# Where an expert's second bias is added: a row matmul on TensorE, or an add on VectorE

## The chip, the cores and the metric

The kernel runs on one core of a Trainium2 chip, in one launch. The metric is the device time in microseconds of an execution; the time shown is the median of three. Besides, one execution was taken by the hardware profiler. Engines are named as in the profile: PE is TensorE's matmuls and PEld its weight loads, DVE is VectorE, ACT is ScalarE, POOL is GpSimd, SP is SyncE. A float32 matmul shows as two rows in the profile.

## The reference

One layer of a graph network over 6250 nodes of 256 features with 206250 edges. The sum of an edge attention (8 heads, softmax over a node's incoming edges) and a linear attention is added to the input; the result is normalised, and a mixture of 8 experts with top-1 routing and a capacity is added. Cut to the part that matters here:

```python
xn = _layernorm(x)
x  = x + gnn(xn, edges) + mix(xn)
h  = _layernorm(x)
probs = softmax(h @ gate_w + gate_b); idx = argmax(probs); prb = probs[idx]
# each token goes to its expert's buffer while there is room (C places)
hmid = relu(einsum('ecd,edf->ecf', buf, w1) + b1[:, None, :])      # 256 -> 1024
ybuf = einsum('ecf,efd->ecd', hmid, w2) + b2[:, None, :]           # 1024 -> 256
x  = x + nan_to_num(ybuf[idx, pos] * (prb * kept))
```

`b2` is the second bias: one row of 256 numbers for each expert, added to every token's result before it is scaled by the token's gate.

## The kernel before

Nodes are sorted by degree and lie in 49 blocks of 128, in three groups of 21, 17 and 11 blocks (`GROUPS`). A key-value table is written first. Then comes the main loop, over the blocks of all groups: each block is cut into units of at most about 20 edge slots, each unit into chunks of 4 or 5 slots. For a chunk, GpSimd gathers 4 or 5 rows of the table for each node (line 662, tile `kvg`, a ring of 10 buffers). VectorE multiplies the keys by the query (line 1620) and reduces to scores (line 1621). When a unit's scores are complete ScalarE takes the exponentials (line 1652, tile `pr`), and while the next unit's chunks are scored, VectorE weights the values of this one (`weigh`, line 1549) and TensorE sums them with an identity matrix into `pa` (line 1553). At a block's end the sum is divided (line 1586) and goes through the output projection, a normalisation and the gate (`out_step`, lines 897 to 952).

All other work is made of Python generators. `background(n)` in the main loop is called twice per chunk with a credit of slots, and takes steps from the first job in `jobs` until the credit is used. Each step says by its `yield` how much it cost. So the engines' queues are written out by hand: where a generator yields is where the attention's instructions come in between, on every engine. A block's own output steps are taken from `outs`.

When all blocks of a group are through, `behind(g)` routes its tokens (`routing`, `to_tiles`) into tiles of one expert each, and `experts(g)` computes them while the next group's attention runs. In the first two groups a tile has 256 rows, two halves of 128 (`SUB` = 2), with 18 and 16 tiles: 34 tiles, 68 halves. In the last group a tile has 128 rows, and there is no attention beside it. Tiles are worked in phases; a phase (0, t) turns the rows and computes `hidden` (line 1369, then the Relu with the first bias on ScalarE at line 1375), a phase (1, t) computes `final`: for each half k, eight matmuls (line 1386) add up in one bank of PSUM, `py`, written out in two parts of four with a yield between. Both parts are followed by `step()`, which takes one step of every open `close`.

`close(t, k, ...)` ends a half: it makes the result tile `res` (pool `d2`, two buffers), scales it by the gate on ScalarE (line 1403, which also leaves a sum for the check on finite numbers), waits some steps, adds the residual rows `xt` on VectorE (line 1406), and one step later stores it, in the first two groups on SyncE to `rbuf` (line 1410). As `final` appends a new `close` to `closing` right ahead of `step()`, its first piece is written out directly after the half's last matmul. The weights `w2_t` (tile `wt`, pool `d3`, three buffers) carry behind them the expert's bias, repeated in all 128 partitions.

The bias comes in one of two ways. In the first two groups a ninth matmul (line 1392) multiplies a row of ones by one row of the bias and adds it to `py`. In the last group, where `last` holds, VectorE adds it (line 1400) before ScalarE scales, and a yield stands between the two.

Of the kernel before, what the change touches and what calls it, by code (L numbers as in the profile page):

```python
# [18 lines left out]
P = 128  # L19
# [51 lines left out]
def gps_layer(  # L71
# [36 lines left out]
    nc = tc.nc  # L108
    N, D = x.shape
# [13 lines left out]
    FC = F // P  # L123
# [33 lines left out]
    with tc.manual_schedule():  # L157
# [12 lines left out]
        ones = keep.tile([P, 8 * max(GROUPS)], F32, name="ones")  # L170
# [52 lines left out]
        def bank(shape):  # L223

            t = bps.tile([P, 512], F32, name="bank")
            n = math.prod(shape)
            v = t[:, :n]
            if len(shape) == 2:
                v = v.rearrange("p (a b) -> p a b", a=shape[0])
            if len(shape) == 3:  # L230
                v = v.rearrange("p (a b c) -> p a b c", a=shape[0], b=shape[1])
            return v
# [616 lines left out]
        def spaced_scatter(key, **kw):  # L849

            s = nc.gpsimd.indirect_dma_start(**kw)
            for other in sent.setdefault(key, []):
                tc.declare_no_dep(s.ins, other.ins, reason="each token has a row of its own")
            sent[key].append(s)
            gap = keep.tile([P, 1], F32, name="gap")
            nc.gpsimd.memset(gap, 0.0)
# [425 lines left out]
        def experts(gi):  # L1282
# [5 lines left out]
            last = gi == NG - 1  # L1288
# [3 lines left out]
            V2 = FC * D  # L1292
# [86 lines left out]
            def final(t, k, part):  # L1379
                w2_t = T[t][1]  # L1380
                w = w2_t[:, :V2].rearrange("p (f d) -> p f d", f=FC)
                if part == 0:
                    T[t]["py"] = bank((D,))
                py = T[t]["py"]
                for f in range(part * FC // 2, (part + 1) * FC // 2):
                    nc.tensor.matmul(  # L1386
                        py, T[t]["hT"][:, f, k * P : (k + 1) * P], w[:, f, :], start=(f == 0),
                        stop=(last and f == FC - 1),
                    )
                if part == 1:  # L1390
                    if not last:
                        nc.tensor.matmul(py, ones[:1, :P], w2_t[:1, V2 : V2 + D], start=False, stop=True)  # L1392
                    closing.append(close(t, k, py, T[t]["xt"][k], w2_t[:, V2 : V2 + D]))

            def close(t, k, py, xt, b2_t):

                f = sum(NSUB[:gi]) + t * SUB + k
                res = d2.tile([P, D], F32, name="res")
                if last:
                    nc.vector.tensor_add(res, py, b2_t)  # L1400
                    py = res
                    yield
                nc.scalar.activation(res, py, AF.Copy, scale=xt[:, D : D + 1], accum_out=finite[:, f : f + 1])  # L1403
                for _ in range(1 if last else 3):
                    yield
                nc.vector.tensor_add(res, res, xt[:, :D])  # L1406
                yield
                if not last:
                    r0 = (t * SUB + k) * P
                    nc.sync.dma_start(rbufs[gi][r0 : r0 + P, :], res)  # L1410
                    return
                spaced_scatter(
                    "out", out=out[:, :],
                    out_offset=bass.IndirectOffsetOnAxis(ap=xt[:, D + 1 :].bitcast(I32), axis=0),
                    in_=res, in_offset=None, bounds_check=N - 1, oob_is_err=False,
                )
# [8 lines left out]
            f = 1.0  # L1425

            def run():
# [19 lines left out]
                for i, (which, t) in enumerate(phases):  # L1447
                    load_w(i + AHEAD)
                    if which == 0:
                        if t > n_begin:  # L1450
                            load(t - 1, "xt", slice(D, XW))
                        for fa in range(0, FC, 2):
                            hidden(t, fa)
                            step()
                            yield 0.9 * SUB * f
                        T[t].pop("xT")
                        turn(t + 1)
                        load_x(t + 2)
                        yield 0.4 * SUB * f
                    else:  # L1460
                        if t == n_end - 1:
                            load(t, "xt", slice(D, XW))
                        for k in range(SUB):
                            for part in range(2):
                                final(t, k, part)
                                step()
                                yield 2.0 * f
                        T[t].clear()
# [755 lines left out]
```

## Time and profile before

| what | value |
|---|---|
| time, median of 3 | 3196.92 us (3190.28 to 3212.74) |
| profiled execution, its own time | 3236.41 us |
| its span | 3234.6 us |
| mean granted TensorE clock | 0.834 |
| busy, PE / DVE / ACT / POOL | 70 / 68 / 24 / 58% of the span |
| L1392, the row matmul | 136 rows of 432 ns (median), two for each of 68 |
| L1403, the scaling, read from PSUM | 68 of 474 ns (median) |
| L1400, the bias add of the last group | 11 of 425 ns (median) |
| L1406, the residual add | 79 of 419 ns (median) |

The times of the table's last four lines are those of the views of these lines. The profile's views read as follows. A group's line gives line, engine, operation, result and operands, then busy time, the mean of one, and the idle time of the engine ahead of it with what ended it. A view of a line gives the least, median and largest duration, who it waited for and who waited for it. A view of stretches gives for each its length, the busy time of each engine with the number of its instructions, and at the end the granted TensorE clock, the DMA engines' share and GB/s. The timeline gives start, length, and in brackets the engine's idle time before. Consecutive rows of one kind are merged there, and rows of different engines overlap.

### The profile page before, as it was taken

To read this page: it belongs to the slowest core of one execution; us is meant where nothing else is said; L and a number is where in the kernel's file an instruction comes from. 1 tells how busy PE (TensorE), PEld (TensorE's weight loads), DVE (VectorE), ACT (ScalarE), POOL (GpSimd) and SP (SyncE) were. 2 spreads that over 40 slices of the span, in tenths; PEclk is the share of its full clock that TensorE was granted. 3 is DMA by queue.
4 is the path that set the end of the run, shared out by engine and by line. 5 is a ranking of instruction groups with operands and counts; after the bars stand their busy time and mean duration, and the time that the engine had idled before them with its cause. 6 is when DMAs were issued, how large, how long until landed. Compare 5 with 4: busy or idle time off the path is not lost. (4 is left out here: it accounts for less than half of the span.)

```text
span 3234.6 us, 29841 instructions
## 1 busy us (share of the span) xinstructions
PE 2256.7 (70%) x8968; PEld 1725.6 (53%) x8968; DVE 2185.8 (68%) x3637; ACT 767.9 (24%) x2022; POOL 1870.4 (58%) x2026
## 2 busy tenths in 40 slices
PE   7635577767777566674468888878745479998847
PEld 3324344545544454553357777666634357776637
DVE  4758788878788577786557667666767546766631
ACT  4200233333333122220012222222210112222213
POOL 4356666666666655655656666656665655665411
PEclk9857788888888788886679998988976689998969
DMA  6556677777776666665767877777664778887475
GB/s 229 183 164 182 210 224 226 226 220 225 222 214 191 190 191 200 205 180 149 256 212 258 262 251 262 245 237 238 209 184 157 249 233 270 288 272 253 155 257 214
DMA packets 257274, 710.88 MB, mean 220 GB/s; under 512 B 42183, under 2 KB 92113, under 8 KB 245580
## 3 DMA queue, kind: packets, MB, share of 16 engines
q0 software_dynamic: 148880, 477.59, 48.6%
q1 hardware_dynamic: 108220, 231.24, 20.2%
q8 instruction: 76, 1.25, 0.2%
q14 instruction: 98, 0.80, 0.1%
HBM read 626.63 MB, written 82.06 MB: 219 GB/s over the span
## 5 line engine op out<-in xcount | busy, mean ns | idle before, releaser
L662 POOL DMA_INDIRECT kvg<-kv_tab,idx x1714 | 1628.6, 950 | 1080.2 <-issue 470.8
L1553 PE MATMUL pa<-kvg,ident 128*128 128x256 f32 x3428 | 1012.1, 451 | 577.0 <-DVE kvg L1549 367.8
L1553 PEld LDWEIGHTS pa<-kvg,ident 128*128 128x128 f32 x3428 | 755.7, 227 | 794.4 <-DVE kvg L1549 407.3
L1620 DVE TENSOR_TENSOR kvg<-kvg,qc 128x1024 f32<-128x1024 f32 (+1 forms) x381 | 514.0, 1349 | 116.0 <-issue 69.2
L1621 DVE TENSOR_REDUCE sim<-kvg 128x32 f32<-128x1024 f32 (+1 forms) x381 | 515.4, 1353 | 18.2 <-remote 4.1
L1549 DVE TENSOR_TENSOR kvg<-kvg,pr 128x1024 f32<-128x1024 f32 (+1 forms) x381 | 510.4, 1343 | 0.0
L1369 PE MATMUL bank<-xTe,wt 128*128 128x256 f32 x1088 | 265.4, 391 | 29.2 <-ACT xTe L1359 15.7
L1386 PE MATMUL bank<-wt,hTe 128*128 128x256 f32 x1088 | 274.8, 399 | 14.9 <-issue 14.7
L1386 PEld LDWEIGHTS bank<-wt,hTe 128*128 128x128 f32 x1088 | 216.8, 202 | 52.1 <-issue 21.2
L1369 PEld LDWEIGHTS bank<-xTe,wt 128*128 128x128 f32 x1088 | 210.7, 197 | 61.8 <-issue 16.9
L1375 ACT ACTIVATE hTe<-bank,wt 128x256 f32<-128x256 f32 x272 | 113.2, 473 | 372.8 <-PE bank L1369 137.1
L756 PE MATMUL bank<-wm,xTm 128*128 128x512 f32 x392 | 185.8, 617 | 3.4 <-issue 3.3
L1560 DVE TENSOR_REDUCE s<-pr 128x8 f32<-128x120 f32 (+8 forms) x108 | 30.5, 282 | 156.6 <-ACT pr L1652 103.3
L756 PEld LDWEIGHTS bank<-wm,xTm 128*128 128x128 f32 x392 | 75.3, 203 | 79.5 <-issue 79.2
L1403 ACT ACTIVATE res<-bank,xt 128x256 f32<-128x256 f32 x68 | 32.2, 474 | 349.0 <-PE bank L1392 183.4
L1578 DVE TENSOR_TENSOR acc<-acc,pa 128x256 f32<-128x256 f32 x59 | 24.9, 421 | 124.7 <-remote 94.2
L548 PE MATMUL pkv<-wn,xT 128*128 128x512 f32 x196 | 95.0, 637 | 16.8 <-DVE kv L562 12.2
L765 ACT ACTIVATE sq<-bank 128x512 f32<-128x512 f32 x98 | 55.5, 594 | 186.1 <-remote 87.9
L785 ACT ACTIVATE ck<-bank,rk 128x64 f32<-128x64 f32 x392 | 86.6, 350 | 30.5 <-issue 15.6
L896 PE MATMUL bank<-ident,qs 128*128 128x128 f32 x56 | 15.0, 358 | 102.3 <-DVE qs L1586 57.6
L773 DVE TENSOR_REDUCE rv<-sq 128x16 f32<-128x1024 f32 x49 | 59.4, 1213 | 38.9 <-ACT sq L765 36.7
L1406 DVE TENSOR_TENSOR res<-res,xt 128x256 f32<-128x256 f32 x79 | 33.3, 421 | 70.2 <-ACT res L1403 41.1
(312 smaller groups left out, 2471.3 us busy)
## 6 DMA issues: line engine op xcount, KB each, us to landing
wt<-in_w_rows_dram SPq DMA_DIRECT2D x34, 1152.0 KB
wt<-in_w_rows_dram SPq DMA_DIRECT2D x34, 1028.0 KB
kvg<-kv_tab,idx POOLq DMA_INDIRECT x1714
xbuf<-zero SPq DMA_DIRECT2D x43, 514.0 KB
kvg<-in_w_rows_dram SPq DMA_DIRECT2D x11, 1152.0 KB
kv_tab<-kv SPq DMA_DIRECT2D x49, 256.0 KB
hx_tab<-hx SPq DMA_DIRECT2D x49, 256.0 KB
kvg<-in_w_rows_dram SPq DMA_DIRECT2D x11, 1028.0 KB
```

Source lines behind the costliest of these rows:

```text
L548: nc.tensor.matmul(done[b], xTs[b // GX][:, b % GX, c, :], wn[:, c, :], start=(c == 0), stop=(c == DC - 1))
L662: nc.gpsimd.indirect_dma_start(out=kv[:, j - j0, :], out_offset=None, in_=kv_tab[:, :], in_offset=bass.IndirectOffsetOnAxis(ap=idx_of[b][: ...
L756: nc.tensor.matmul(pm, xT_of[b][:, c, :], wmf[:, c, s * MI : (s + 1) * MI], start=(c == 0), stop=(c == DC - 1),)
L773: nc.vector.tensor_reduce(rv, sqs[b], AX.X, ALU.add)
L785: nc.scalar.activation(cks[b][:, h, :], pms[b][0][:, h * MD : (h + 1) * MD], AF.Copy, scale=rk[:, h : h + 1])
L1369: nc.tensor.matmul(ph[:, k, :], w[:, c, f * P : (f + 1) * P], T[t]["xT"][:, c, :size], start=(k == 0 and c == 0), stop=(k == 1 and c == DC ...
L1375: nc.scalar.activation(T[t]["hT"][:, f, :size], ph[:, k, :], AF.Relu, bias=w1_t[:, V1 + f : V1 + f + 1])
L1386: nc.tensor.matmul(py, T[t]["hT"][:, f, k * P : (k + 1) * P], w[:, f, :], start=(f == 0), stop=(last and f == FC - 1),)
L1549: nc.vector.tensor_tensor(vals, vals, v["pr"][:, j0 - s0 : j1 - s0, :, None].to_broadcast([P, m, GH, GD]), ALU.mult)
L1553: nc.tensor.matmul(v["pa"], ident, kv[:, j, D:], start=(j0 + j == s0), stop=(j0 + j == s1 - 1),)
L1620: nc.vector.tensor_tensor(keys, keys, qc[:, None, :].to_broadcast([P, j1 - j0, D]), ALU.mult)
L1621: nc.vector.tensor_reduce(sim[:, j0 - s0 : j1 - s0, :], keys.rearrange("p j (h d) -> p j h d", d=GD), AX.X, ALU.add)
```

## The change

The ninth matmul goes, and `close` adds the bias on VectorE in all groups, as the last group did already; the yield between the add and ScalarE's scaling comes with it. ScalarE then reads `res` instead of PSUM. All that follows in `close` is written out one step later. The adds of the last group stay as they were.

```diff
                 for f in range(part * FC // 2, (part + 1) * FC // 2):
                     nc.tensor.matmul(
                         py, T[t]["hT"][:, f, k * P : (k + 1) * P], w[:, f, :], start=(f == 0),
-                        stop=(last and f == FC - 1),
+                        stop=(f == FC - 1),
                     )
                 if part == 1:
-                    if not last:
-                        nc.tensor.matmul(py, ones[:1, :P], w2_t[:1, V2 : V2 + D], start=False, stop=True)
                     closing.append(close(t, k, py, T[t]["xt"][k], w2_t[:, V2 : V2 + D]))
 
             def close(t, k, py, xt, b2_t):
 
                 f = sum(NSUB[:gi]) + t * SUB + k
                 res = d2.tile([P, D], F32, name="res")
-                if last:
-                    nc.vector.tensor_add(res, py, b2_t)
-                    py = res
-                    yield
+                nc.vector.tensor_add(res, py, b2_t)
+                py = res
+                yield
                 nc.scalar.activation(res, py, AF.Copy, scale=xt[:, D : D + 1], accum_out=finite[:, f : f + 1])
                 for _ in range(1 if last else 3):
                     yield
                 nc.vector.tensor_add(res, res, xt[:, :D])
                 yield
```

## The prediction

> **What bounds the kernel now.** I read the page first, for the totals; then the busy time in the two stretches in which the first two groups' experts run (they are where the page's lines L1369 and L1386 work on `wt`); then the row matmul's own view; then the timeline around single closes, because busy shares cannot show who waits for whom. By "close" I mean the end of one 128-row result, 68 of them in the first two groups.
>
> ```profile
> span 3234.6 us, 29841 instructions
> PE 2256.7 (70%) x8968; PEld 1725.6 (53%) x8968; DVE 2185.8 (68%) x3637; ACT 767.9 (24%) x2022; POOL 1870.4 (58%) x2026
> 1690.00:2340.00 650.00, 547.12 (x2349) 446.51 (x2348) 449.11 (x649) 147.53 (x355) 404.45 (x427) 0.92 0.76 245
> 2600.00:3060.00 460.00, 412.05 (x1805) 338.81 (x1806) 291.31 (x419) 112.12 (x281) 257.01 (x272) 0.94 0.75 250
> ```
>
> The columns of the last two lines are length, PE, PEld, DVE, ACT, POOL, then the granted clock. In these 1110 us TensorE is busy 959 us and idle only 151; VectorE is busy 740 and idle 370. Over the whole span the two look alike (70% and 68%); here TensorE is the tight engine. So on shares alone this change is a gain: work leaves the tight engine for the slack one. What decides is the order.
>
> ```profile
> L1392 PE MATMUL bank<-wt,ones x136: 371/432/610, 1700.7 to 3049.9; 1*128 1x256 f32 x136
>   ACT res L1403: 183.4, 34
> L1400 DVE TENSOR_TENSOR res<-bank,kvg x11: 424/425/425, 3149.4 to 3219.1; 128x256 f32<-128x256 f32 x11
> L1549 DVE TENSOR_TENSOR kvg<-kvg,pr 128x1024 f32<-128x1024 f32 (+1 forms) x381 | 510.4, 1343 | 0.0
> ```
>
> The first two lines are from the view of line 1392: two rows for each row matmul, and ScalarE, not VectorE, is who waited for it, 183 us in 34 long waits. ScalarE is 22 to 24% busy there, so that waiting was nearly free. The third line is the same add in the last group, the price of what is added. The last is one chunk's weighting, without which TensorE's sums of that chunk (L1553) cannot start.
>
> Now one close, from the timeline (start, length, what):
>
> ```profile
> 1870.56 1.21 DVE L1549 TENSOR_TENSOR kvg<-kvg,pr 128x1024 f32<-128x1024 f32 x1
> 1871.68 1.21 DVE L1620 TENSOR_TENSOR kvg<-kvg,qc 128x1024 f32<-128x1024 f32 x1
> ...
> 1875.60 1.19 DVE L1549 TENSOR_TENSOR kvg<-kvg,pr 128x1024 f32<-128x1024 f32 x1
> ...
> 1877.76 1.89 PE L1386 MATMUL bank<-wt,hTe 128*128 128x256 f32 x8
> ...
> 1879.58 0.69 PE L1392 MATMUL bank<-wt,ones 1*128 1x256 f32 x2
> 1880.21 1.99 PE L1386 MATMUL bank<-wt,hTe 128*128 128x256 f32 x8
> 1880.32 0.47 ACT L1403 ACTIVATE res<-bank,xt 128x256 f32<-128x256 f32 x1 [6.46 <-PE bank L1392]
> ...
> 1882.04 1.89 PE L1553 MATMUL pa<-kvg,ident 128*128 128x256 f32 x8
> ```
>
> VectorE runs some 8 us ahead: it had finished the weighting by 1876.8 that TensorE takes up at 1882.04. That lead keeps TensorE fed. In the changed program's order this close's add stands between the first two DVE lines, at 1871.77, and needs the sum that TensorE ends at 1879.65.
>
> **The change, part by part.**
>
> *Row matmul removed.* 68 pairs. In the timeline what follows a pair starts 0.62 us after it (1879.58 to 1880.21), so 68 x 0.62 = **42 us** less TensorE work. It fell due on the tight engine, so I credit all of it; 0 is the other end.
>
> *Add on VectorE.* 68 x 0.425 = 29 us of VectorE time. Beside 370 idle us this alone would hide.
>
> *The wait that the add brings.* `step()` runs right after the matmuls are written out, so the add goes into VectorE's queue at once. I compared, for all 68 closes, the end of the VectorE instruction ahead of the add with the end of the last L1386 row of that sum. In 64 VectorE would arrive early, by 6.7 us on average over all (456 us in sum); in 4 it is up to 1.5 us late and waits for nothing. While it waits, everything behind it stands: the next product, reduction and weighting, hence TensorE's next L1553, and behind that the gathers that want the freed slot. ScalarE's exponentials (L1652) wait likewise for VectorE's scores.
>
> The 456 us are not the loss: TensorE works while VectorE waits. The loss begins when TensorE is done with the sum and the weighting it needs next has yet to be made. For each close I added the measured durations of the VectorE work from the add through that weighting (call it D), plus 0.15 us for the two hand-overs (an engine starts 0.04 us after TensorE's end at 1880.32; the way back is of that order), and took off S, the time from the sum's end to the start of that L1553 in the trace, row matmul included. The result is net of the 42 us:
>
> - 29 closes have the weighting right behind the add. D = 0.425 + 1.34 and some small work, 1.80; S = 0.75, for L1553 follows at once. 1.95 - 0.75 = 1.20 each, **+35 us**.
> - 32 have product, reduction and weighting behind it. D = 0.425 + 3 x 1.34 + 0.9 of small operations = 5.33; S = 3.61, since TensorE has other expert matmuls meanwhile. 5.48 - 3.61 = 1.87 each, 60 us; no single close can gain more than its row matmul, and that floor makes it **+63 us**. The close shown: D 5.08, S 2.38, so +2.85.
> - 3 at a block's end have the query chain (L1586, then L896) behind it: 4.59 + 0.15 - 1.60 = 3.15 each, **+9 us**.
> - 4 are not late: **0**.
>
> Sum **+107 us**, net. Ends: a waiting VectorE also spares it later waits (in the first stretch 43 us for L1652), and if half of the 107 returns that way it is +50; if the lead that is lost at each close also lengthens TensorE's gap at block boundaries by 1 us at some 35 of them, +142. I take 107, since nothing else feeds TensorE and both engines shift together.
>
> *The clock.* Longer TensorE gaps meet the clock gate. The rows:
>
> ```profile
> 2700.00:2800.00 100.00, 95.89 (x440) 80.64 (x439) 69.45 (x98) 26.48 (x67) 60.10 (x65) 0.98 0.84 282
> 3000.00:3100.00 100.00, 74.49 (x316) 59.40 (x315) 60.88 (x110) 20.85 (x46) 34.67 (x37) 0.85 0.40 126
> ```
>
> At 96% busy the grant is 0.98, at 74% it is 0.85. After the change TensorE has 959 - 42 = 917 us in 1110 + 107 = 1217 us, 75%; by the rows the mean grant goes from 0.93 to about 0.85, and 917 x (0.93/0.85 - 1) = 86 us if all of it is on the path. The Trainium skill, "TensorE: Matmul & The Clock Gate", Part 1, ties half speed to an idle window of about 3.4 us: by that only gaps over 3.4 us count, 13 of my 68, and with half of a cold stretch lost (they last mostly 6.8 us in the trace, so 3.4) 44 us. Part of slow TensorE time lies beside VectorE work. I take **+25**; 0 and 86 are the ends.
>
> *What moves with it.* The scaling (L1403), the second add (L1406) and the store (SyncE, L1410) come one step later, half a chunk or about 3 us. ScalarE no longer waits for TensorE at L1403; the work behind it (L933, L1375, L1652) is hidden by its 76% idle time or depends on the same TensorE progress. SyncE's 68 stores slip past other loads and stores of that half chunk by about 3 us; the result is gathered only after the group is done. The `wt` slot is held until the add has read the bias, 0.46 us beyond the sum; three slots hide that. The sum's bank comes free sooner. `res` has two buffers: only in the last two closes of each group does an add wait for a store to land. 0 to 10 us; I take **+3**. GpSimd's order is unchanged.
>
> Sum: 107 + 25 + 3 = **+135 us**. Against the profiled execution (3236.4, its span 3234.6) that is about 3371. The profiled one is 39.5 us above the median of the runs, and the shift is carried over: 3196.9 + 135 = **3332 us**.
>
> **Rivals.**
>
> *Faster.* TensorE's backlog in 2700 to 2900 us is deep (lateness 9 to 14 us at several closes, 96% busy). If such a backlog stood everywhere, TensorE would have at least D (1.8 to 5.3 us) of other work after each sum, VectorE's wait would cost nothing, and the row matmuls' 42 us would be gained, with some 8 us of ScalarE's unblocking: 3147. It decides from S > D + 0.15 on. Against it: S is 0.55 at more than 20 closes, L1553 coming directly after the sum. 0.04.
>
> *No difference.* The gaps shrink to about the 42 us saved, because VectorE's other waits (370 idle us) give back the rest: 3197. For it: much of that idle time is ScalarE-bound. Against: it lies at block ends, not behind the closes. 0.07.
>
> *Heavier.* Cold clock at its full 86 us and the boundary loss: 142 + 86 = +228, 3425. For it: cold stretches already follow gaps in the trace. Against: VectorE's time covers part. 0.20.
>
> That the change does something else than said I exclude: the changed program has 68 adds more and 68 row matmuls fewer.
>
> **How the numbers follow.** The forecast has 0.69, the heavier 0.20, no difference 0.07, faster 0.04. About 1% (32 us) is what a measurement of this kernel can tell from no change. Slower by over 1%: 0.69 + 0.20 = 0.89; within 0.07; faster 0.04. The range goes from +44 (only the 29 and the 3 closes behind which TensorE has next to nothing else to do, no cold clock) to the heavier case: 3241 to 3425.
>
> **What would show it.** In the changed profile: no L1392; L1400 with 79 rows of 0.42 us; VectorE waiting for L1386 ahead of L1400 by some 300 us or more; ScalarE's wait at L1403 for TensorE gone; "PE pa L1553 <- DVE kvg" in these stretches up from 50 us (36 + 14) by about 100; granted clock there 0.86 to 0.91; time up to 1690 us unchanged and the two stretches longer by about 75 and 55. Wrong if L1553's waits for the weighting do not grow: then TensorE was fed from elsewhere, and the first or second rival holds.

## The result, and the profile after

The changed kernel is **slower**: 3361.5 us, median of four (3350.2 to 3368.6), against 3193.6 of before in the same session; ratio 1.051, 95% interval 1.0477 to 1.0543. The profiled execution took 3361.96 us. Lines below the edit have numbers three smaller than before: the bias add is L1397, the weighting L1546, TensorE's sum of a chunk L1550.

From the page after:

```profile
span 3360.1 us, 29640 instructions
PE 2256.0 (67%) x8832; PEld 1738.7 (52%) x8832; DVE 2205.8 (66%) x3705; ACT 771.4 (23%) x2022; POOL 1874.6 (56%) x2026
...
L1550 PE MATMUL pa<-kvg,ident 128*128 128x256 f32 x3428 | 1056.2, 466 | 730.7 <-DVE kvg L1546 537.0
...
L1397 DVE TENSOR_TENSOR res<-bank,wt 128x256 f32<-128x256 f32 x68 | 28.9, 425 | 417.9 <-PE bank L1386 213.4
```

The line of TensorE's sums from the page before:

```profile
L1553 PE MATMUL pa<-kvg,ident 128*128 128x256 f32 x3428 | 1012.1, 451 | 577.0 <-DVE kvg L1549 367.8
```

TensorE has 136 rows fewer and is busy for the same time. VectorE has 68 rows more, 28.9 us of work, and was idle 417.9 us just ahead of them; the profile puts 213.4 us of that down to line 1386, the sum. The idle time of TensorE ahead of L1550 that ended with a weighting grew from 368 us (L1553 before) to 537. From the view of waits after (us, times, longest):

```profile
PE pa L1550 <- DVE kvg L1546: 537.0, 147, 23.2
DVE res L1397 <- PE bank L1386: 282.6, 47, 36.5
...
ACT res L1400 <- DVE res L1397: 81.1, 16, 11.5
```

ScalarE's wait for TensorE at the scaling (183 us before) is gone from this view, and VectorE waits for TensorE in its place. The 36.5 us belong to the last group.

The two stretches of the experts, each from its first `hidden` matmul to its last `final` matmul (length, PE, PEld, DVE, ACT, POOL, granted clock, DMA share, GB/s):

```profile
1637.10:2367.90 730.80, 564.58 (x2316) 468.36 (x2316) 456.05 (x673) 151.23 (x363) 404.71 (x427) 0.88 0.69 219
2638.60:3173.30 534.70, 420.58 (x1773) 352.09 (x1771) 296.59 (x442) 116.56 (x286) 265.16 (x279) 0.90 0.68 223
```

The same cut of before:

```profile
1655.10:2310.20 655.10, 557.59 (x2386) 457.35 (x2386) 438.33 (x629) 150.15 (x362) 397.62 (x419) 0.91 0.74 242
2581.80:3049.30 467.50, 415.29 (x1835) 342.79 (x1833) 289.40 (x417) 113.85 (x286) 264.33 (x279) 0.94 0.76 255
```

So the stretches grew by **76 and 67 us**. The part between them stayed (272 and 271), the tail nearly too (185 and 187), and the part ahead was 18 us shorter (1655 and 1637). That part is untouched by the change; in four other kernels profiled on a chip of equal speed it took 1635 to 1645, so the profiled execution of before was long there. It was 43 us longer in all than the median of its kernel, and the one of after was at its median; hence the spans differ by 126 us and the medians by 168. Some 10 to 20 of the 43 us lie in the part ahead. Where the others lie is not shown, so the stretches' growth may be somewhat more than 76 and 67.

The close that the prediction showed, in the timeline after:

```profile
1866.84 1.21 DVE L1546 TENSOR_TENSOR kvg<-kvg,pr 128x1024 f32<-128x1024 f32 x1
...
1870.90 3.62 PE L1386 MATMUL bank<-wt,hTe 128*128 128x256 f32 x16
...
1872.83 0.42 DVE L1397 TENSOR_TENSOR res<-bank,wt 128x256 f32<-128x256 f32 x1 [4.77 <-PE bank L1386]
1873.17 1.21 DVE L1617 TENSOR_TENSOR kvg<-kvg,qc 128x1024 f32<-128x1024 f32 x1
1874.41 1.22 DVE L1618 TENSOR_REDUCE sim<-kvg 128x32 f32<-128x1024 f32 x1
...
1876.56 1.19 DVE L1546 TENSOR_TENSOR kvg<-kvg,pr 128x1024 f32<-128x1024 f32 x1
...
1877.80 2.51 PE L1550 MATMUL pa<-kvg,ident 128*128 128x256 f32 x8 [3.28 <-issue]
```

VectorE is done with the weighting at 1868.05 and stands still for 4.77 us, until the first eight rows of 1870.90 are through (the other eight are the next half's). Then come product, reduction and small work, and only at 1877.75 is the next weighting ready. TensorE had run out of work at 1874.52 and stands idle for 3.28 us, to 1877.80. (The profile names no releaser for this row, "issue"; that it waited for the weighting is read from the 0.05 us between the two.) This is the handing-back of a stall: TensorE makes VectorE wait, and then the VectorE work that was held up makes TensorE wait.

### The profile page after: what moved, and what is told of

It is laid out like the page before. It is cut to its first block, busy times and chain, and to the rows that moved or that the text cites. A ratio compares the mean times of both kernels' runs of the same rounds, so it can differ in the third digit from the quotient of the medians.

```text
span 3360.1 us, 29640 instructions
## 1 busy us (share of the span) xinstructions
PE 2256.0 (67%) x8832; PEld 1738.7 (52%) x8832; DVE 2205.8 (66%) x3705; ACT 771.4 (23%) x2022; POOL 1874.6 (56%) x2026
## 5 line engine op out<-in xcount | busy, mean ns | idle before, releaser
L1550 PE MATMUL pa<-kvg,ident 128*128 128x256 f32 x3428 | 1056.2, 466 | 730.7 <-DVE kvg L1546 537.0
L1550 PEld LDWEIGHTS pa<-kvg,ident 128*128 128x128 f32 x3428 | 778.9, 234 | 963.8 <-DVE kvg L1546 598.8
L1546 DVE TENSOR_TENSOR kvg<-kvg,pr 128x1024 f32<-128x1024 f32 (+1 forms) x381 | 510.4, 1343 | 0.0
L1397 DVE TENSOR_TENSOR res<-bank,wt 128x256 f32<-128x256 f32 x68 | 28.9, 425 | 417.9 <-PE bank L1386 213.4
L1369 PEld LDWEIGHTS bank<-xTe,wt 128*128 128x128 f32 x1088 | 217.5, 202 | 48.5 <-ACT xTe L1359 16.2
L1649 ACT ACTIVATE pr<-sim 128x120 f32<-128x120 f32 (+8 forms) x108 | 30.0, 277 | 230.4 <-DVE sim L1647 144.9
L504 POOL DMA_INDIRECT part<-in_dst_dram,row_i x49 | 46.4, 948 | 54.3 <-DVE cnt L499 20.6
```

Of the source, the lines that this page charges most:

```text
L1369: nc.tensor.matmul(ph[:, k, :], w[:, c, f * P : (f + 1) * P], T[t]["xT"][:, c, :size], start=(k == 0 and c == 0), stop=(k == 1 and c == DC ...
L1546: nc.vector.tensor_tensor(vals, vals, v["pr"][:, j0 - s0 : j1 - s0, :, None].to_broadcast([P, m, GH, GD]), ALU.mult)
L1550: nc.tensor.matmul(v["pa"], ident, kv[:, j, D:], start=(j0 + j == s0), stop=(j0 + j == s1 - 1),)
```

## The experiments

Each is compared with the kernel before on its own chip. The first four ran on a chip on which before took 3199.1 us; the other eight on two chips on which it took 2759.6 and 2760.8 us, so only ratios and differences are carried across. The result above, with before at 3193.6 us, belongs to the first speed. Step numbers are the generator's: one step is one round of `step()`, about half a chunk.

**e1: the wait alone.** To the kernel before a copy is added:

```diff
                     py = res
                     yield
+                else:
+                    seen = d2.tile([P, 1], F32, name="seen")
+                    nc.vector.tensor_copy(seen, py[:, :1])
```

> The row matmul stays and ScalarE scales as before; added is only a copy of one column of the sum by VectorE, at the place in VectorE's order where the changed kernel has its add. Wait theory (the loss is TensorE starved behind a VectorE that waits for the finished sum): the gaps come back in full and the row matmul is not saved, so at least as slow as the changed kernel: before + 150 to 200 us, about 3345 to 3395. Work theory (the 29 us of adds or ScalarE's longer path cost it): a column costs 68 x 0.1 us, so before + 0 to 20.

Measured: ratio **1.0523** (1.047 to 1.0576), about +167 us. The profiled execution took 3400.8 us, some 30 us above the median of this kernel's others, so the idle times that it shows may be somewhat high. Groups of instructions (busy, mean ns, idle before):

```profile
L1556 PE MATMUL pa<-kvg,ident 128*128 128x256 f32 x3428 | 1073.7, 472 | 695.2 <-DVE kvg L1552 499.9 <-issue 191.5 <-DVE hx L1251 2.0
L1405 DVE COPY seen<-bank 128x1 f32<-128x1 f32 x68 | 10.8, 158 | 454.8 <-PE bank L1392 266.1 <-remote 86.7 <-issue 57.9
L1406 ACT ACTIVATE res<-bank,xt 128x256 f32<-128x256 f32 x68 | 32.2, 474 | 423.8 <-DVE seen L1405 279.8
```

68 copies of one column, 10.8 us of work, cost as much as the whole change. VectorE stands idle 454.8 us ahead of them, TensorE 500 us for the weighting. The wait is the cause, not the add. One more thing changed: the last line shows that ScalarE's scaling now comes behind the copy. That is hardly the cause, for in e4 and e12 below it stays behind the add and nearly all of the loss is gone.

**e2: the work alone.** To the kernel before an add is added that does not need the sum:

```diff
                     py = res
                     yield
+                else:
+                    nc.vector.tensor_add(res, b2_t, b2_t)
```

> The row matmul stays; added is VectorE's add of 256 columns at the same place, but of the bias with itself, into the result tile that ScalarE then overwrites, so it does not wait for the sum. Wait theory: hidden in VectorE's idle time, before + 0 to 30 us (29 us if every one of them were on the path). Work theory: most of the changed kernel's loss, before + 100 or more.

Measured: ratio 1.0063 (1.0037 to 1.009), +17 us between the medians. It also ties ScalarE's scaling to VectorE, so 17 us is an upper price for the work. The work theory is out.

**e3: neither matmul nor add.** The second bias of the first two groups is left out.

```diff
-                        stop=(last and f == FC - 1),
+                        stop=(f == FC - 1),
...
-                    if not last:
-                        nc.tensor.matmul(py, ones[:1, :P], w2_t[:1, V2 : V2 + D], start=False, stop=True)
```

> The second bias is left out in the first two groups: no row matmul, no add. It measures what the row matmul is worth. Prediction's term: 68 x 0.62 = 42 us on the tight engine, so before - 42, about 3152. If TensorE's time there is not on the path: before - 0 to 15.

Measured: ratio 0.9964 (0.9944 to 0.9984), **-13 us**, where the prediction had credited 42. It is also the right base for what the add costs, for its matmuls are the changed kernel's. Its two stretches:

```profile
1638.50:2284.30 645.80, 525.90 (x2316) 446.87 (x2316) 445.28 (x640) 148.97 (x362) 403.06 (x426) 0.91 0.76 250
2552.30:3009.30 457.00, 397.53 (x1773) 338.73 (x1772) 289.02 (x417) 114.43 (x286) 263.72 (x279) 0.94 0.78 261
```

The same 4089 TensorE rows as in the changed kernel, in 1102.8 us instead of 1265.5. Of the 162.7 us between them, TensorE's idle time is 280.3 - 179.4 = 101, and the same rows lasting longer are 985.2 - 923.4 = 62.

**e4: the add one step later.**

```diff
+                for _ in range(0 if last else 1):
+                    yield
                 res = d2.tile([P, D], F32, name="res")
                 nc.vector.tensor_add(res, py, b2_t)
                 py = res
                 yield
                 nc.scalar.activation(...)
-                for _ in range(1 if last else 3):
+                for _ in range(1 if last else 2):
```

> The changed kernel with one step put ahead of the add and one taken off the three after the scaling. Laid against the trace of before, VectorE would then reach the add on average 2.6 us early in place of 6.7, and 221 us in sum in place of 456. Wait theory: about half of the gross loss (the 42 us saved stand against it) goes, before + 20 to + 80. Work theory: as the changed kernel, before + 165.

Measured: ratio 1.0036 (1.0013 to 1.0059), **+11 us**, under the expected 20 to 80.

```profile
L1552 PE MATMUL pa<-kvg,ident 128*128 128x256 f32 x3428 | 1011.9, 451 | 604.9 <-DVE kvg L1548 395.8 <-issue 205.8 <-DVE hx L1251 2.7
L1399 DVE TENSOR_TENSOR res<-bank,wt 128x256 f32<-128x256 f32 x68 | 28.8, 423 | 195.8 <-PE bank L1386 76.3 <-remote 38.3 <-issue 34.7
```

VectorE still stands idle for 195.8 us ahead of the add, nearly half of the changed kernel's 417.9, and little of it costs time: TensorE's wait for the weighting is at 395.8 near the 367.8 of before. Against the kernel without the bias (e3) it is +24 us, not far from the 17 that e2 gave for the work. So the loss does not go with the waiting time, as I had expected here. The reading that fits, and that e12 bears out, is that TensorE's other work covers a short wait of VectorE, and only what goes beyond that is lost.

**e5: two steps later, and the second add close behind.** As e4, with 2 and 1 for the two counts of steps, so that the residual add follows the scaling by one step.

> The changed kernel with two steps put ahead of the add and two taken off after the scaling. Laid against the trace of before, VectorE would reach the add 1.8 us after the sum on average; what is early sums to 69 us in place of 456. Wait theory: the wait is nearly gone and the row matmul is saved, before - 30 to + 20. Work theory: before + 165. If the longer hold of the sum's bank bites, slower than that by TensorE's waits for a bank.

Measured: ratio 1.015 (1.0125 to 1.0176), +42 us: a miss. From the view of waits:

```profile
DVE res L1405 <- ACT res L1402: 179.1, 61, 7.8
...
DVE res L1399 <- PE bank L1386: 96.3, 20, 36.8
```

The wait at the bias add is mostly gone, but the two steps came out of the three behind the scaling, and now VectorE waits 61 times at the residual add (L1405) for ScalarE. In the changed kernel on a chip of that speed (e9) that wait is 22.2 us. The bank's longer hold, which I had named as a risk, does not appear in the view. So the same fault seems to appear at a new place; no run of its own shows that these waits are the 42 us.

**e6 and e10: the bias folded into the residual rows.** `res = gate * sum + (gate * bias + x)`, with the bracket made without the sum.

```diff
+                else:
+                    nc.vector.scalar_tensor_tensor(
+                        xt[:, :D], b2_t, xt[:, D : D + 1], xt[:, :D], op0=ALU.mult, op1=ALU.add
+                    )
```

(and no row matmul, as in e3)

> No row matmul; VectorE multiplies the bias by the gate and adds it to the residual rows (one operation, all operands in SBUF, no wait for the sum), at the place where the changed kernel has its add; ScalarE scales the sum as before. The check on finite numbers then sees the result without the bias. Wait theory: the row matmul's gain less what of 29 us of VectorE work is not hidden, before - 42 to - 10. Work theory: before + 100 or more.

> The bias folded into the residual rows, once more. Wait theory: no loss on either chip, before - 30 to + 5. On the first chip, where leaving the row matmul out gained 13 us and an add without a wait cost 20, it should be within 1% of before; on the second it was 22 us faster.

Measured: 0.9911 (0.9887 to 0.9935), -22 us, and 0.9906 (0.9883 to 0.9929), **-26 us**. The VectorE work (68 of 479 ns in e10) is somewhat more than the changed kernel's and stands at the same place in its queue, yet it does not wait for the sum. All that it waits for is the loading of its rows, in e10:

```profile
DVE xt L1402 <- DMA xt<-xbuf: 28.0, 5, 19.0
```

This version beats both kernels there. It was not run on the first chip, and its check on finite numbers sees the result without the bias.

**e7: fillers in the gaps.** The changed kernel with three matmuls behind each of the 68 adds in the program's order.

```diff
                 py = res
+                if not last:
+                    fill = bank((D,))
+                    for j in range(3):
+                        nc.tensor.matmul(fill, ident, b2_t, start=(j == 0), stop=(j == 2))
                 yield
```

> The changed kernel with three more matmuls of 256 columns per close, of the identity with the bias, into a bank that nobody reads, queued on TensorE directly after the sum (about 1.4 us each close, 97 us in all). Wait theory: they fall mostly into the gaps that TensorE has there anyway (1.9 us and more at most closes), so the changed kernel + 0 to 50, and the granted clock in the two stretches comes back towards 0.90 or more. If the cold clock is a large part of the loss: faster than the changed kernel by 20 or more. If TensorE has no gaps there: the changed kernel + 97.

Measured: 1.055 (1.052 to 1.0581), +155 us; the changed kernel (e9, the other chip of that speed) has 1.0591 (1.0562 to 1.0619). So 204 matmuls more cost nothing. The stretches of e7:

```profile
1392.70:2031.10 638.40, 563.97 (x2526) 477.31 (x2527) 455.24 (x673) 150.09 (x362) 410.19 (x431) 0.95 0.78 255
2251.60:2738.80 487.20, 431.18 (x1959) 366.92 (x1958) 296.82 (x442) 117.09 (x286) 277.33 (x292) 0.95 0.76 251
```

TensorE is busy 60.7 us longer than in e9 (below), and the stretches are 12.8 us shorter: the fillers lie in gaps. The grant is up from 0.93 to 0.95. The intervals of the two ratios overlap, so a gain of some 12 us from the clock is possible and not shown.

**e8: the first group alone.** The condition for `stop` becomes `(last or gi == 0) and f == FC - 1`; the row matmul is made only where `gi == 1`, and the add where `gi != 1`.

> The change in the first group alone (36 of the 68 closes); the second keeps its row matmul. By the prediction's sum 64 of the 107 us and half of the clock's 25 fall to the first group: before + 75, the second stretch as long as before. In the changed kernel's trace the first stretch grew by 76 us: the same number. If the two stretches' losses hang together, another.

Measured: 1.0406 (1.0381 to 1.0431), **+115 us**, not 75. Its first stretch is 648.0 us long, that of the changed kernel on a chip of that speed (e9) 645.6. So the first group's loss does not hang on the second's, and there it makes up 115 of 166 us; in the profiles on the slower chip it was 76 of 143.

**e9, e11, e12: changed kernel, no bias, add one step later, side by side with e10.**

> The changed kernel once more, as the reference for the runs beside it on the same chip. On the first chip it took 1.051 of before. On the second chip (before 2760 us) the change in the first group alone already cost 115 us. Wait theory: there VectorE and TensorE are nearer to being the only bound, so the loss is larger in us: + 170 to + 210, about 1.06 to 1.08. If it is the first chip again: 1.05.

> The bias left out in the first two groups, once more. What the row matmul is worth: 13 us on the first chip, in place of the prediction's 42. If TensorE is held up there by something that its rows do not show, the second chip should give the larger gain, 25 to 45 us; if the row matmul's time is simply beside the path, 15 or less on both.

> The add one step later, once more. On the first chip it took back nearly all of the loss (before + 12). Wait theory on the second chip: at most a third of the changed kernel's loss stays, + 0 to + 60.

Measured, before 2760.8 us: changed 2926.5, ratio **1.0591** (1.0562 to 1.0619), +166; no bias 0.9894 (0.9873 to 0.9915), -28; one step later 0.9946 (0.9927 to 0.9965), **-15**. Stretches of e9, then of e11:

```profile
1394.60:2040.20 645.60, 530.14 (x2315) 445.31 (x2316) 456.18 (x674) 150.89 (x363) 409.68 (x431) 0.93 0.77 252
2256.70:2749.50 492.80, 404.32 (x1772) 340.31 (x1771) 297.17 (x443) 117.26 (x286) 278.10 (x292) 0.93 0.75 249
```

```profile
1392.60:1918.50 525.90, 493.96 (x2315) 426.97 (x2316) 444.40 (x639) 150.22 (x362) 398.03 (x420) 0.98 0.89 304
2137.80:2555.50 417.70, 377.76 (x1772) 328.67 (x1771) 289.55 (x418) 115.26 (x286) 277.08 (x292) 0.95 0.86 293
```

1138.4 us against 943.6: 194.8 us, of which 132 are idle time of TensorE (203.9 against 71.9) and 63 are rows that last longer (934.5 against 871.7). TensorE's sums in e9, e11 and e12:

```profile
L1550 PE MATMUL pa<-kvg,ident 128*128 128x256 f32 x3428 | 1006.8, 449 | 550.4 <-DVE kvg L1546 545.6
L1551 PE MATMUL pa<-kvg,ident 128*128 128x256 f32 x3428 | 974.2, 438 | 434.7 <-DVE kvg L1547 433.9
L1552 PE MATMUL pa<-kvg,ident 128*128 128x256 f32 x3428 | 972.4, 438 | 442.8 <-DVE kvg L1548 438.8
```

In e12 VectorE still stands idle for 148 us ahead of the add (348 in e9), but TensorE waits for the weighting hardly longer than without any bias, and the time is 14 us above e11's. Moving one `yield` ahead of the add turns +166 into -15. Two expectations were missed: e9 was to lose 170 to 210 us, and e12 was not to be faster than before.

## Why the prediction was right, step by step

The forecast was 3332 us, in a range from 3241 to 3425; measured are 3361.5.

- **The mechanism.** VectorE reaches the add early, its queue stands, and TensorE lacks its next weighting. Shown by e1 (the wait without the change: +167 us) against e2 (the work without the wait: +17), and by e6 and e10 (the work at the same place without the wait: faster than before).
- **The forecast of signs in the profile.** VectorE waiting for the sum ahead of the add by 300 or more: it was idle for 418 us, but the profile puts only 213 down to the sum's matmuls (321 of 348 on the faster chip), so this sign is met on the slower chip by the idle time alone. ScalarE's wait at the scaling gone: yes. L1553's waits for the weighting in the two stretches, 50 us, up by about 100: 103 and 70 us, up by 124. Grant 0.86 to 0.91: 0.88 and 0.90. Stretches longer by 75 and 55: 76 and 67.
- **The gaps.** With the credit taken out, they were sized at 107 + 42 = 149 us. Against the kernel without bias TensorE's idle time grew by 101 us on the first chip and 132 on the other: the right size, somewhat high.
- **The clock** was sized at 25, with 0 and 86 as ends; the same matmuls' rows last 62 and 63 us longer. Too low, if all of that is on the path; no run shows how much is. The 86 came from two stretches of before, from which a grant of 0.85 at 75% busy was read; after the change it was 0.88 and 0.90 at 77 and 79%. The trace of e9 records the clock at half speed 33 times in its two stretches, 161 us in sum, that of e11 7 times, 56 us. The rule that was weighed (the Trainium skill, "TensorE: Matmul & The Clock Gate", Part 1: half speed follows an idle window of about 3.4 us) gave an estimate of 44 us, by counting gaps over 3.4 us alone. That count was too narrow: 18 of the 33 begin with no TensorE gap of that length in the 7 us before them, so shorter gaps count too.
- **Gross loss.** 149 + 25 + 3 = 177 us by the prediction. Measured from no bias to changed: 1.051 - 0.9964 = 0.0546 of 3197, 175 us; on the other chip 2926.5 - 2732.5 = 194. That 177 and 175 agree is luck: on the first chip the gaps were sized 48 us too high, and the clock 37 too low if all of it counts.
- **The step that was mis-sized: the credit of 42 us for the row matmul.** It took TensorE, as the tight engine, to be worth its full time. Leaving the matmul out gains 13 us there (e3) and 28 on the other chip (e11). That difference, 29 us, is nearly all that the forecast of +135 lacks to the measured +168: the result lies between the likeliest case and the heavier one. Nothing measured asks for the heavier rival's price for block boundaries: TensorE's idle time grew by less than the 149 us without it.
- **The rivals.** "Faster" needed TensorE to have other work behind each sum. The kernel with the add one step later shows what that takes: with half a chunk's delay the cover nearly suffices, and then on the faster chip the change gains 15 us. The lateness expected for this version from the trace of before, 221 us in sum, was to leave half of the gross loss; 24 of 175 us were left, and 14 of 194 on the faster chip. "No difference" fell with the result: the medians differ by 168 us and TensorE's waits for the weighting grew.

## What to carry to other kernels

Here an instruction that read another engine's fresh result held up everything behind it in its own engine's queue. So price the move by what the waiting engine feeds, not by busy shares: 29 us of work beside 370 us of idle time cost 166 to 168 us. Put such a reader half a chunk later (one `yield`: +11 and -15 us), or reshape the sum so that the operand is ready early (the fold: -26 us on the faster chip); and look that the wait does not turn up at the next reader (e5). A busy share of 86% does not make every microsecond taken off that engine a gain: 42 us of matmuls were worth 13 and 28.

## What the runs showed of the hardware that I had not expected

The same kernel before took 3199 us on one chip and 2760 and 2761 on two others. In the part ahead of the experts, the same in all these kernels, it is 1635 to 1655 us in the six profiles of the slower speed against 1391 to 1397 in the eight on the faster chips. In the traces of the slower speed TensorE's readers often start late. From the timeline of before:

```profile
2710.81 1.89 PE L1369 MATMUL bank<-xTe,wt 128*128 128x256 f32 x8
...
2716.33 0.84 ACT L1375 ACTIVATE hTe<-bank,wt 128x256 f32<-128x256 f32 x2 [6.64 <-PE pa L1553]
```

The Relu needs the rows that by the trace end at 2712.70, and starts 3.6 us later. The first two groups have 136 such pairs of Relus. In before 39 of them start over 1 us after both the last row that they need and ScalarE's work ahead of them have ended, in e4 32, and none in e6, e8, e9 and e11. The ends of matmul rows in the profile are modelled, so the rows themselves cannot tell what TensorE did in that time, and the split into idle and busy time is less sure on the slower chip than on the faster ones. It would explain why the row matmul was worth less there, but no run takes it apart, and its cause stays open.
